# Sixteen MLP passes on one core: which second-layer products are cut in quarters, and the order of the sums around them

## The chip, the cores and the metric

The kernel runs on one core of a Trainium2 chip, as one launch. The metric is the device time in microseconds (us). A core has five engines that matter here, each with its own queue that is worked off in order: TensorE (PE, with its weight loads PEld), VectorE (DVE), ScalarE (ACT), GpSimd (POOL) and SyncE (SP, which issues most DMAs). They meet only through semaphores.

## The reference, cut to what matters

Eight samples of 512 tokens by 512 features go through four stages: a grid update, an attention block with its MLP, a mixture-of-experts MLP (one expert per sample) and a low-rank response. The change touches the two MLPs and what runs between them:

```python
h = _ln(x) * g2 + beta2
ff = _gelu2(h @ W1 + b1) @ W2 + b2          # x + ff, W1: 512 x 2048, W2: 2048 x 512
...
h = gelu(einsum('bsh,bhi->bsi', x, Wi[expert]) + bi[expert])
o = einsum('bsi,bih->bsh', h, Wo[expert]) + bo[expert]
y = layernorm(o + x) * gamma + beta
...
return hidden_states + strength * response  # strength: one number per sample; response: rank 32
```

All of it is in 32-bit floats.

## The kernel before, in words

The first half of the span is the grid and the attention. The second half is `mlp_stage` (L1198): 16 passes, `run(q, hooks)` for q = 0 to 15; 0 to 7 are the attention block's MLP for the eight samples, 8 to 15 the experts' MLP. Each pass multiplies with seven products in place of eight (Strassen's scheme in Winograd's form: sums of quadrants are formed first, then seven products of half size, then sums of the products).

**First layer**, steps 0 to 27: four groups g of 512 hidden features, seven products each (`L1`, L1592), every step one product. W's quadrant sums come from `w_quads` (L1570, POOL, four sums a group), the activations' from `b_staged` (L1510). The outcome lands in `acts`, and ACT applies the GELU in place.

**Second layer**, steps 28 to 55: seven products over all four groups, four steps each. Call the left quadrants of `acts` A and the right ones of `wo` B, with the sums S1 to S4 and T1 to T4. The order before is P1 = A00 B00 (28), P5 = S1 T1 (32), P2 = A01 B10 (36), P6 = S2 T2 (40), P7 = S3 T3 (44), P3 = S4 B11 (48), P4 = A11 T4 (52); in the last pass P3 and P7 change places, and P4 is done by rows for the kernel's end.

- `second` (L1784) does one product in halves: 16 matmuls that are 256 wide, into one PSUM bank. Before, P1, P5 and P6 go this way.
- `third` (L1802) does one product in quarters, with a second level of the same scheme: 28 matmuls that are 128 wide, into two banks (a and b), and an epilogue: ACT copies a piece of a to `yw`, DVE makes three sums in `yw`, ACT copies one piece to b, DVE adds `yw` to b. Before, P2, P7, P3 and P4 go this way. Each needs four sums on its left side (`l_sum`, L1665: DVE, with three copies by ACT into a staging bank, `stage`) and four on its right side (`r_sum`, L1654: POOL). `PLACES` (L1633) says in which quadrants of `acts` and `wo` its operands lie, `set_up` and `fresh` which buffers take the sums.
- `s13` and `t13` (L1614, L1888) form S1 and S3, T1 and T3. `t2s2` (L1698) forms T2 and S2 in place of T1 and S1, called behind each group of P5. `t4s4` (L1706) forms T4 in B00's place and S4 in A00's.

**The order of the work around the matmuls** is written out by hand: `hooks[s]` is a list of functions called when PE's program comes to step s. A hook fixes the place of its instructions in their own engine's queue; only data ties them to PE. Hooks registered earlier come first within a step. Those that `mlp_stage`'s loop registers (L2158 on) come before those of `run`.

**PSUM**: eight banks. Tag "u" has six (products of both layers and the small products `pf`, `pg`, `pz`, `po`), tag "tr" has two (all copies of `stage`).

**Side work in a pass.** Passes 0 to 7: four Gram-Schmidt steps, each `gs_norm` (DVE, a square root on POOL) and `gs_b` (DVE, then `gs_a`: POOL issues two DMAs that spread the next row, `qb`); the next sample's layer norm (`norm` at 21, `normed` at 31) and its transposes (`rows32` at 34 to 37), with `turn` at 38. Passes 9 to 15: the finishing of the pass before, `tail_norm` (5), `tail_normed` (9), transposes (14 to 20), `tail_spread` (28), `tail_scale` (34 to 37, ACT), `tail_gamma` (37, one DVE product over 2048 columns), `tail_feats` (38, `pf`), `gate` (39, `pg`), `strength` (41, `pz`, then ACT's sigmoid with a table load, then DVE), `add_beta` (42, DVE and four POOL sums), `tail_sum` (46, four `po` in four banks), `tail_add` (47 to 51, DVE).

**Loads**: `load_wo` (step 0, 4 MB), `load_wi` of groups 2 and 3 (step 0) and of the next pass's 0 and 1 (48 and 52), into the buffers x0 to x3, which between them hold the sums of the quartered products.

Of the kernel before, what the change touches and what calls it, by code (L numbers as in the profile page):

```python
# [11 lines left out]
F32 = mybir.dt.float32  # L12
# [8 lines left out]
NB = 8  # L21
# [1176 lines left out]
def mlp_stage(tc, a, small, xp, io, wo8, x1d, ident, eidx, sigs, layernorm, rstd_of, phalf, wl3, g2, b1, first):  # L1198
# [4 lines left out]
    with ExitStack() as ctx:  # L1203
# [211 lines left out]
        def norm(q):  # L1415
            st = small.tile([P, R, 6], F32, name=f"ln1_st_{q}", tag="ln1_st")
            mv = small.tile([P, R, 2], F32, name=f"ln1_mv_{q}", tag="ln1_mv")
            for r in range(R):
                pin(nc.vector.bn_stats(st[:, r, :], xs[q][:, r, :]))
                pin(nc.vector.bn_aggr(mv[:, r, :], st[:, r, :]))  # L1420
            norms[q] = mv, rstd_of(mv[:, :, 1], LN_EPS, R, "ln1", pin)

        def normed(q):
            mv, rs = norms.pop(q)
            h = [ap.tile([P, D], F32, name=f"h_{q}_{r}", tag="tmp", bufs=4) for r in range(R)]
            sh = small.tile([P, R], F32, name=f"ln1_s_{q}", tag="ln1_s")
            pin(
                nc.vector.scalar_tensor_tensor(sh, mv[:, :, 0], -1.0, rs, ALU.mult, ALU.mult)
            )
            for r in range(R):  # L1430
                pin(
                    nc.scalar.activation(
                        h[r], xs[q][:, r, :], AF.Identity, bias=sh[:, r : r + 1],
                        scale=rs[:, r : r + 1],
                    )
                )
            hs[q] = h

        blks = {}

# [154 lines left out]
        def run(q, hooks):  # L1595
# [26 lines left out]
            def fresh(*ks):  # L1622
# [8 lines left out]
                    hx[k] = v  # L1631

            PLACES = {  # L1633
                "p2": ((0, 1), (1, 0)), "p7": ((1, 0), (0, 1)), "p3": ((0, 0), (1, 1)),
                "p4": ((1, 1), (0, 0)),
            }

            def left(key, k, m):
# [26 lines left out]
            def l_sum(key, n):  # L1665
# [8 lines left out]
                else:  # L1674
                    add(s2, s1, st[key + "b"], sub)
                    add(s4, st[key + "c"], s2, sub)

            def set_up(part):
                if part == 0:
                    fresh(2)  # L1680
                    r_homes("p2", *hx[2])
                elif part == 1:
                    fresh(0, 1, 3)
                    l_homes("p2", *hx[3])
                    r_homes("p7", *hx[0][0:3])
                    r_homes("p3", *hx[1][0:3])
                elif part == 2:
                    fresh(2, 3)
                    l_homes("p7", hx[0][3], hx[1][3], hx[2][0])
                    r_homes("p4", *hx[2][1:4])  # L1690
                    l_homes("p3" if last else "p4", *hx[3][0:3])
                elif not last:
                    l_homes("p3", *(
                        io.tile([P, NG, P], F32, name=f"s4_{q}_{i}", tag=f"v{i}", bufs=2)
                        for i in range(3)
                    ))

            def t2s2(g):  # L1698
                if g < NG - 1:
                    stage(f"s2_{g + 1}", act_quad(g + 1, 0, 0))  # L1700
                else:
                    stage("s4_0", act_quad(0, 0, 1))
                gadd(ts[q, g], quad(wo[:, g], 1, 1), ts[q, g], ALU.subtract)
                add(ss[g], ss[g], st[f"s2_{g}"], ALU.subtract)

            def t4s4(g):  # L1706
                if g < NG - 1:
                    stage(f"s4_{g + 1}", act_quad(g + 1, 0, 1))
                gadd(quad(wo[:, g], 0, 0), quad(wo[:, g], 1, 0), ts[q, g], ALU.subtract)
                add(act_quad(g, 0, 0), st[f"s4_{g}"], ss[g], ALU.subtract)  # L1710

            tail, last = q > NB, q == NQ - 1
            four = (40, 41, 42), (44, 45, 46)
            for part, s in enumerate((25, 28, 40, 44)):
                at(hooks, s, set_up, part)
            for key, ss_, ts_ in (
                ("p2", (28, 29, 30), (25, 26, 27, 28)),
                ("p7", four[last], (29, 30, 31, 31)),
                ("p3", four[not last], (40, 40, 40, 40) if tail else (40, 41, 42, 43)),
                ("p4", (47, 48, 49), (44, 44, 44, 44) if tail else (43, 44, 45, 46)),  # L1720
            ):
                if key == "p4" and last:
                    continue
                for n_, s in enumerate(ss_):
                    at(hooks, s, l_sum, key, n_)
                for n_, s in enumerate(ts_):
                    at(hooks, s, r_sum, key, n_)
            for g in range(NG):
                at(hooks, 36 + g, t4s4, g)

            for g in range(NG):
                out = {
# [48 lines left out]
                        gelu(0)  # L1781


            def second(s, A, B, each=None):  # L1784
                y = ps.tile([P, 2, H], F32, name=f"y_{q}_{s}", tag="u", bufs=6)
                for g in range(NG):
                    go(s + g)
                    if s == 28 and g == 2:
                        stage(f"s13_{NG - 1}", act_quad(NG - 1, 1, 0))
                    if s == 28 and g == 3:  # L1790
                        s13(NG - 1)
                    for i in range(2):
                        for m in range(2):
                            mm(
                                y[:, m, :], A(g)[:, i, m * P : (m + 1) * P], B(g)[:, i, :],
                                g + i + m == 0, g + i + m == NG + 1,
                            )
                    if each:
                        each(g)
                return y  # L1800

            def third(s, key):  # L1802
# [14 lines left out]
                    a=((L(0, 0), M(0, 0)), (s2, t2), (s3, t3), (s1, t1)),  # L1817
                    b=((L(1, 0), M(1, 0)), (s4, M(1, 1)), (L(1, 1), t4)),
                )
                jobs = [(n, k, g, v) for n in "ab" for k, v in enumerate(four[n]) for g in range(NG)]  # L1820
                for i, (n, k, g, (A, B)) in enumerate(jobs):
                    if i % 7 == 0:
                        go(s + i // 7)
                    last = len(four[n]) - 1
                    mm(
                        ys[n][:, k, :], A[:, g, :], B[:, g, :], k + g == 0,
                        k == last and g == NG - 1,
                    )
                    if n == "a" and k == last and g == NG - 1:
                        pin(nc.scalar.copy(w[:, 0, :], y[:, 0, :]))  # L1830
                        add(w[:, 1, :], y[:, 1, :], w[:, 0, :])
                        add(w[:, 2, :], y[:, 2, :], w[:, 1, :])
                        add(w[:, 1:4:2, :], y[:, 3:4, :].to_broadcast([P, 2, P]), w[:, 1:3, :])
# [15 lines left out]
            p1 = second(28, lambda g: act_quad(g, 0, 0), b(0, 0))  # L1849
            pin(nc.scalar.copy(yu, p1))  # L1850
            x_add(0, 0, p1)
            stage("s2_0", act_quad(0, 0, 0))
            p5 = second(32, lambda g: ss[g], lambda g: ts[q, g], t2s2)
            x_add(1, 1, p5)
            x_add(0, 1, p5)
            p2 = third(36, "p2")
            x_add(0, 0, p2)
            p6 = second(40, lambda g: ss[g], lambda g: ts[q, g])
            add(p6, p6, yu)
            x_add(0, 1, p6)  # L1860
            pin(nc.scalar.copy(yu, p6))
# [8 lines left out]
            if q < NQ - 1:  # L1870
                p4 = third(52, "p4")
                x_add(1, 0, p4)
            else:
                for m in range(2):
                    y = ps.tile([P, H], F32, name=f"y_{q}_52_{m}", tag="u", bufs=6)
                    for g in range(NG):
                        if g % 2 == 0:
                            go(52 + 2 * m + g // 2)
                        for i in range(2):
                            mm(  # L1880
                                y, act_quad(g, 1, 1)[:, i, m * P : (m + 1) * P],
                                b(0, 0)(g)[:, i, :], g + i == 0, g + i == NG,
                            )
                    last_row(m, y)

# [272 lines left out]
        for q in range(NQ):  # L2158
# [18 lines left out]
            at(hooks, 7, w_quads, q, 2, gadd)  # L2177
            at(hooks, 14, w_quads, q, 3, gadd)
            for g in range(NG):
                at(hooks, 18 + 2 * g, t13, q, g)  # L2180
            if nx:
                if nx < NB:
                    at(hooks, 21, norm, nx)
                    at(hooks, 31, normed, nx)
                for r in range(R):
                    at(hooks, 34 + r, lambda r=r, n=nx: rows32(
                        n, r, hs[n][r] if n < NB else xs[n][:, r, :]
                    ))
                at(hooks, 38 if q <= NB else 40, turn, nx)
                if nx < NB:  # L2190
                    for c in range(KC):
                        at(hooks, 46 + c, scale, nx, c)
                at(hooks, 51, b_staged, nx)
                at(hooks, 51, w_quads, nx, 0, gadd)
# [13 lines left out]
            elif q > NB:  # L2208
# [6 lines left out]
                at(hooks, 28, tail_spread, o)  # L2215
                for c in range(KC):
                    at(hooks, 34 + c, tail_scale, o, c)
                at(hooks, 37, tail_gamma, o, every)
                at(hooks, 38, tail_feats, o, every)
                at(hooks, 39, gate, o)  # L2220
                at(hooks, 41, strength, o)
# [100 lines left out]
```

## Time and profile before

| | us |
|---|---|
| three runs | 2627.62, 2633.33, 2635.84 (median 2633.33) |
| the profiled execution | 2628.13 |
| its span, first to last instruction | 2626.3 |
| PE busy | 2586.3 (98%) |
| DVE busy | 2015.7 (77%) |
| POOL busy | 1753.4 (67%) |
| ACT busy | 1309.0 (50%) |

The granted TensorE clock is 0.996 of full speed. In a listing of groups a line gives the source line, the engine, the operation, the output and inputs by the program's names, the count and the busy time. In a timeline or a chain a line begins with the start in us and the duration; a bracket holds the idle time of the engine before it and what ended it. A 32-bit matmul shows as two records, so a product in halves is 32 records and one in quarters 56. `y` is a product in halves, `y_36a` and `y_36b` the banks of the quartered product that begins at step 36; `u` is the first layer; `q` and `s` among inputs are buffers of sums.

### The profile page before, as it was taken

What the parts mean: (1) busy time and instruction counts of PE and PEld (TensorE: products, weight loads), DVE (VectorE), ACT (ScalarE), POOL (GpSimd) and SP (SyncE); (2) the same over time, 40 slices, a digit from 0 to 9 for tenths busy, and PEclk for the clock granted to TensorE, in tenths of its full rate; (3) what the DMA queues carried; (4) which work ended last, traced back from release to release, by engine and by line L of the source; (5) the groups of instructions that cost most, each with busy time, mean ns of one, the idle gap of its engine ahead of it and who ended that gap; (6) DMA issues with size and microseconds to landing.
All of it is one profiled execution on the core that took longest, in us unless ns stands there. A gap on an engine that the chain in (4) does not pass through costs nothing.

```text
span 2626.3 us, 44146 instructions
## 1 busy us (share of the span) xinstructions
PE 2586.3 (98%) x15664; PEld 1962.4 (75%) x15664; DVE 2015.7 (77%) x3924; ACT 1309.0 (50%) x2743; POOL 1753.4 (67%) x1422
## 2 busy tenths in 40 slices
PE   6999999999999999999999999999999999999998
PEld 3455555555555555798999899899899899889897
DVE  7978798888888756588877778777567667667667
ACT  2676767676777766243344334333334434434433
POOL 4555565655555656488787887877676786776773
PEclk9999999999999999999999999999999999999999
DMA  9775766666767555544553563564345355256241
GB/s 330 255 235 182 262 200 236 217 230 217 250 222 241 171 165 197 145 135 101 167 181 71 153 197 78 128 191 141 112 155 189 101 185 199 91 185 208 83 169 44
DMA packets 242128, 460.60 MB, mean 175 GB/s; under 512 B 33936, under 2 KB 77528, under 8 KB 232822
## 3 DMA queue, kind: packets, MB, share of 16 engines
q1 hardware_dynamic: 238042, 447.04, 49.7%
q0 software_dynamic: 3552, 10.72, 4.2%
q8 instruction: 125, 2.05, 0.3%
q14 instruction: 93, 0.76, 0.1%
q10 hardware_dynamic: 316, 0.03, 0.0%
HBM read 398.43 MB, written 55.09 MB: 173 GB/s over the span
## 4 chain that ended last, share of the span: by engine, by line
PE 93%; DVE 2%; issue 2%; DMA 2%; ACT 1%; POOL 0%; SPq 0%; DVEq 0%; ACTq 0%; POOLq 0%
PE u L1211 29%; PE y L1211 13%; PE tr L564 8%; PE s L561 5%; PE pv L561 4%; PE ctx L561 4%; PE pk L561 4%; PE pq L561 4%; PE o L561 3%; PE y_44a L1211 2%; PE y_36a L1211 2%; PE y_48a L1211 2%; PE y_52a L1211 2%; PE y_36b L1211 2%; PE y_44b L1211 2%
## 5 line engine op out<-in xcount | busy, mean ns | idle before, releaser
L998 POOL TENSOR_TENSOR bt<-bt,mk 128x1024 f32<-128x1024 f32 x256 | 541.6, 2140 | 58.3 <-DMA bt<-in_bias 38.0
L1026 ACT ACTIVATE bt<-bt,mn 128x512 f32<-128x512 f32 x512 | 365.7, 718 | 78.7 <-DVE mn L1021 78.5
L564 PEld LDWEIGHTS tr<-ident,bt 128*128 128x128 f32 x2048 | 230.4, 141 | 148.8 <-issue 101.7
L1021 DVE CUSTOM_DVE_ANT_0 bt<-s,bt 128x512 f32<-128x512 f32 x512 | 329.7, 683 | 4.7 <-PE s L561 3.6
L1211 PE MATMUL u<-bt,wi 128*128 128x256 f32 x1440 | 330.5, 379 | 0.0
L1052 ACT COPY pt<-tr 128x512 f32<-128x512 f32 x376 | 207.6, 584 | 204.5 <-PE tr L564 196.6
L1211 PEld LDWEIGHTS u<-bt,wi 128*128 128x128 f32 x1440 | 272.4, 190 | 36.4
L1217 DVE TENSOR_TENSOR act<-u,u 128x512 f32<-128x512 f32 x256 | 174.7, 687 | 158.7 <-PE u L1211 121.1
L564 PE MATMUL tr<-ident,bt 128*128 128x128 f32 x2048 | 277.5, 278 | 7.7 <-ACT pt L1052 3.4
L1211 PE MATMUL u<-tb,ws 128*128 128x256 f32 x1024 | 242.3, 379 | 0.0
L1211 PE MATMUL y<-t,s 128*128 128x256 f32 x1024 | 228.1, 380 | 0.0
L1741 ACT ACTIVATE act<-act,b 128x512 f32<-128x512 f32 x128 | 84.1, 713 | 285.7 <-DVE act L1217 268.2
L1211 PEld LDWEIGHTS u<-tb,ws 128*128 128x128 f32 x1024 | 194.2, 190 | 26.8 <-issue 0.3
L1211 PEld LDWEIGHTS y<-t,s 128*128 128x128 f32 x1024 | 192.7, 190 | 25.6 <-issue 0.4
L1741 ACT ACTIVATE act<-act,bi 128x512 f32<-128x512 f32 x128 | 84.6, 713 | 244.1 <-DVE act L1217 244.1
L1050 DVE COPY pt<-tr 128x512 f32<-128x512 f32 x136 | 93.7, 689 | 133.6 <-PE tr L564 132.9
L561 PE MATMUL s<-kt,qt 32*128 32x512 f32 x1024 | 164.1, 640 | 1.0 <-ACT kt L651 0.8
L1217 DVE TENSOR_TENSOR u<-u,u 128x512 f32<-128x512 f32 x192 | 130.9, 682 | 43.7 <-PE u L1211 43.5
L1220 POOL TENSOR_TENSOR q<-wo,q 128x512 f32<-128x512 f32 x126 | 160.4, 1273 | 5.0
L1220 POOL TENSOR_TENSOR wo<-wo 128x512 f32<-128x512 f32 x111 | 143.3, 1291 | 8.7
L1220 POOL TENSOR_TENSOR t<-wo,t 128x512 f32<-128x512 f32 x64 | 80.9, 1279 | 101.0 <-PE y L1211 100.9
L1503 ACT COPY st_s<-act 128x512 f32<-128x512 f32 x192 | 111.9, 589 | 70.4 <-DVE s L1217 32.2
(443 smaller groups left out, 5604.9 us busy)
## 6 DMA issues: line engine op xcount, KB each, us to landing
bt<-in_bias SPq DMA_DIRECT2D x256, 512.0 KB
wo<-in_W SPq DMA_DIRECT2D x32, 1024.0 KB
wi<-in_Wi SPq DMA_DIRECT2D x32, 1024.0 KB
wo<-in_Wo_e SPq DMA_DIRECT2D x32, 1024.0 KB
wi<-in_W SPq DMA_DIRECT2D x28, 1024.0 KB
td<-tt SPq DMA_DIRECT2D x22, 1024.0 KB
bt<-td SPq DMA_DIRECT2D x176, 128.0 KB
gq<-coef_q SPq DMA_DIRECT2D x21, 512.0 KB
```

The costliest lines, as they stand in the source:

```text
L561: pin(nc.tensor.matmul(out, lhsT=lhsT, rhs=rhs, start=start, stop=stop))
L564: pin(nc.tensor.transpose(out, src, ident))
L998: nc.gpsimd.tensor_tensor(bt, bt, mask[b, r][:, None, :].to_broadcast([P, 2, S]), ALU.add)
L1021: nc.vector.tensor_tensor_reduce(bt[:, i, :], ss[h], bt[:, i, :], -1.0, 3.0e38, ALU.add, ALU.min, mn)
L1026: nc.scalar.activation(bt[:, i, :], bt[:, i, :], AF.Exp, bias=mn, scale=-1.0, accum_out=sums[b, c][:, h, r : r + 1],)
L1050: pin(nc.vector.tensor_copy(pt[:, :, r % 2, :], tr))
L1052: pin(nc.scalar.copy(pt[:, :, r % 2, :], tr))
L1211: pin(nc.tensor.matmul(out, lhsT=lhsT, rhs=rhs, start=start, stop=stop))
L1217: pin(nc.vector.tensor_tensor(out, x, y, op))
L1220: pin(nc.gpsimd.tensor_tensor(out, x, y, op))
L1503: pin(nc.scalar.copy(t, parts[0]))
L1741: nc.scalar.activation(acts[:, g, k, :], acts[:, g, k, :], func, bias=bi[:, j : j + 1])
```

## The change

- P6 is done in quarters by `third` (step 40); with P2, P7, P3 and P4 that makes five. P2 moves from 36 to 32, P5 from 32 to 36. The order is P1, P2, P5, P6, P7, P3, P4.
- S2 is written to A00's place and T2 to B00's (`s2` at 31 to 34, `t2` at 30 to 33); S4 to A01's and T4 to B10's (`s4` at 39 and 40, `t4` at 37 to 40). P6, P3 and P4 read them there.
- Buffers of the second-level sums are shared out anew (`set_up` in five parts, `free` for the buffers that S1 and T1 leave).
- In `third` the products of bank a come in the order 0, 2, 3, 1.
- POOL's list: `t13` at 10, 11, 16, 18 (before 18, 20, 22, 24); P2's right sums at 20 to 23 (before 25 to 28), P7's at 23 to 26 (before 29 to 31), P6's at 33 to 36, P3's at 40 to 43, P4's at 44 to 47; in passes 9 to 15 P3's at 40, 40, 41, 41 and P4's at 46, 46, 47, 48.
- `normed` is called by row at 33 to 36 (before all at 31); `tail_gamma` at 22 (before 37).

```diff
             PLACES = {
-                "p2": ((0, 1), (1, 0)), "p7": ((1, 0), (0, 1)), "p3": ((0, 0), (1, 1)),
-                "p4": ((1, 1), (0, 0)),
+                "p2": ((0, 1), (1, 0)), "p6": ((0, 0), (0, 0)), "p7": ((1, 0), (0, 1)),
+                "p3": ((0, 1), (1, 1)), "p4": ((1, 1), (1, 0)),
             }
...
-            def t2s2(g):
...
+            def t2(g):
+                o = quad(wo[:, g], 0, 0)
+                gadd(o, quad(wo[:, g], 1, 1), ts[q, g], sub)
+
+            def s2(g):
+                o = act_quad(g, 0, 0)
+                add(o, ss[g], st[f"s2_{g}"], sub)
                 if g < NG - 1:
                     stage(f"s2_{g + 1}", act_quad(g + 1, 0, 0))
...
+            def t4(g):
+                o = quad(wo[:, g], 1, 0)
+                gadd(o, o, quad(wo[:, g], 0, 0), sub)
+
+            def s4(*gs_):
+                for g in gs_:
+                    o = act_quad(g, 0, 1)
+                    add(o, st[f"s4_{g}"], act_quad(g, 0, 0), sub)
...
-            for part, s in enumerate((25, 28, 40, 44)):
+            for part, s in enumerate((20, 28, 36, 40, 44)):
                 at(hooks, s, set_up, part)
+            for g in range(NG):
+                at(hooks, 30 + g, t2, g)
+                at(hooks, (37, 37, 38, 39)[g] if tail else 37 + g, t4, g)
             for key, ss_, ts_ in (
-                ("p2", (28, 29, 30), (25, 26, 27, 28)),
-                ("p7", four[last], (29, 30, 31, 31)),
-                ("p3", four[not last], (40, 40, 40, 40) if tail else (40, 41, 42, 43)),
-                ("p4", (47, 48, 49), (44, 44, 44, 44) if tail else (43, 44, 45, 46)),
+                ("p2", (28, 29, 30), (20, 21, 22, 23)),
+                ("p6", (36, 37, 38), (33, 34, 35, 36)),
+                ("s4", (), ()),
+                ("p7", four[last], (23, 24, 25, 26)),
+                ("p3", four[not last], (40, 40, 41, 41) if tail else (40, 41, 42, 43)),
+                ("p4", (47, 48, 49), (46, 46, 47, 48) if tail else (44, 45, 46, 47)),
             ):
+                if key == "s4":
+                    at(hooks, 30, stage, "s2_0", act_quad(0, 0, 0))
+                    for g in range(NG):
+                        at(hooks, 31 + g, s2, g)
+                    at(hooks, 38, s4_stage, 0, 1)
+                    at(hooks, 39, s4, 0, 1)
+                    at(hooks, 39, s4_stage, 2, 3)
+                    at(hooks, 40, s4, 2, 3)
+                    continue
...
-            for g in range(NG):
-                at(hooks, 36 + g, t4s4, g)
...
+                turns = dict(a=(0, 2, 3, 1), b=(0, 1, 2))
...
-            stage("s2_0", act_quad(0, 0, 0))
-            p5 = second(32, lambda g: ss[g], lambda g: ts[q, g], t2s2)
+            p2 = third(32, "p2")
+            x_add(0, 0, p2)
+            p5 = second(36, lambda g: ss[g], lambda g: ts[q, g])
             x_add(1, 1, p5)
             x_add(0, 1, p5)
-            p2 = third(36, "p2")
-            x_add(0, 0, p2)
-            p6 = second(40, lambda g: ss[g], lambda g: ts[q, g])
+            p6 = third(40, "p6")
             add(p6, p6, yu)
...
-                at(hooks, 18 + 2 * g, t13, q, g)
+                at(hooks, (10, 11, 16, 18)[g], t13, q, g)
             if nx:
                 if nx < NB:
                     at(hooks, 21, norm, nx)
-                    at(hooks, 31, normed, nx)
+                    for r in range(R):
+                        at(hooks, 33 + r, normed, nx, r)
...
-                at(hooks, 37, tail_gamma, o, every)
+                at(hooks, 22, tail_gamma, o, every)
```

## The prediction

> **What bounds the kernel now.** I read the page's shares and chain first, then the chain in order of time, then the timelines of the engines in one middle pass (1356 to 1455 us) and one late pass (2021 to 2122 us).
>
> ```profile
> PE 93%; DVE 2%; issue 2%; DMA 2%; ACT 1%; POOL 0%; SPq 0%; DVEq 0%; ACTq 0%; POOLq 0%
> ...
> 1356.86 48.35 PE u L1211 x224
> 1405.21 13.81 PE y L1211 x64
> 1419.02 3.57 PE y_36a L1211 x32
> 1422.59 2.68 PE y_36b L1211 x24
> 1425.27 6.91 PE y L1211 x32
> ```
>
> PE sets the end: 93% of the chain. A pass is 48.35 us of first layer and seven second-layer products one behind the other, with no gap. A product in halves (y) is 32 matmul records in 6.91 us, 216 ns each; one in quarters (y_36a with y_36b) is 56 in 6.25 us, 111.6 ns each. Passes 1 to 7 take 94.08 us (1356.86 to 1450.94), passes 9 to 14 take 97.67 (2021.73 to 2119.39): there pf, pg, pz and po of the pass before are let in, and again PE has no gap. So nothing is to be won but matmul time; anything late on DVE, ACT or POOL can only add.
>
> **The gain.** P6 goes from halves to quarters: 6.91 - 6.25 = 0.66 us, in all 16 passes 10.6 us. The four other quartered products, P1 and P5 keep their records; only their order changes. The sums for S2, T2, S4 and T4 keep their number too (four of each a pass, DVE and POOL): they go to other places at other steps, and the last pass's last product reads T4 from its new place.
>
> The Trainium skill, "TensorE: Matmul & The Clock Gate", Back-to-back issue gap, speaks against quarters: the spacing of matmuls with weight loads falls only from 131 ns at width 512 to 81 at 128. Read linearly (an estimate from that page) 128 would cost 0.83 of 256, so 56 records 10.0 us, and the change would lose 3.1 us a pass, 50 us in all. The rows above have 0.517 and decide.
>
> **What the extra quarters cost elsewhere.** Per pass four POOL sums (1.28 us each), four DVE sums on the left (0.60 apart), three ACT copies, and the epilogue: an ACT copy, three DVE sums (1.07), an ACT copy, a DVE sum (0.56). DVE gets 4.0 us more behind the first layer. Between its first p2 sum and its last x sum the middle pass has 44 us with about 6.4 idle, the late pass 49 with about 7. That fits on paper; whether it stalls is a matter of order, so I laid the queues out by hand, in program order, with the rows' durations. Zero is 48.35 us before a pass's first second-layer matmul (1356.69 and 2021.56).
>
> **Late passes.** PSUM has six "u" banks. At step 46 four po tiles are taken while P7 holds two, so every bank of P6 must be free by then. P6 had one bank; now its second bank is held until yu is copied out of it.
>
> ```profile
> 2094.10 1.28 ACT L2020 ACT_TABLE_LOAD   x1
> 2095.39 0.26 ACT L2020 ACTIVATE st<-pz,gb 128x1 f32<-128x1 f32 x1
> 2095.69 0.16 DVE L1217 TENSOR_TENSOR st<-st,sigs 128x1 f32<-128x1 f32 x1 [1.03 <-ACT st L2020]
> ...
> 2099.41 0.70 DVE L1217 TENSOR_TENSOR y<-y,yu 128x512 f32<-128x512 f32 x1 [0.28 <-PE y L1211]
> 2100.14 0.69 DVE L1217 TENSOR_TENSOR x<-y,x 128x512 f32<-128x512 f32 x1
> 2100.92 0.59 ACT L1861 COPY yu<-y 128x512 f32<-128x512 f32 x1 [3.26 <-DVE x L1217]
> ...
> 2102.43 1.14 PE L1211 MATMUL po<-rw,ft 32*128 32x512 f32 x8
> ```
>
> Before, P6's bank is free at 2101.51 and po starts at 2102.43: 0.9 us to spare. After: P5 ends at 68.43 plus pf 1.1 and pg 0.81, so 70.34; P6 takes 6.25 and pz 0.14, to 76.73; step 46 is half of P7 later, 79.85, and its third po at 80.4. DVE: two x sums from 70.5, then s4 of groups 2 and 3, to 73.03. Only then does ACT get the staging bank for p7b (0.6), then the table load (1.28) and the sigmoid: 75.25. DVE waits for it in order at st, and behind it stand s1, s3, beta, s2, s4 (3.2 us, to 78.5), P6's three sums (79.5), an ACT copy (0.3), the sum to y (0.6), with yu (0.74), x (0.7), and ACT's yu copy: 82.5. PE waits 2.1 us. P3's first bank needs P7's three sums, which end at 86.75 with P7's matmuls over at 86.3: 0.45 more. I take 2.5 us a pass, in seven passes 17.6; bounds 0.8 (DVE a microsecond and a half earlier) and 3.5. The gamma product (2.29 us of DVE, 0.59 of ACT), moved from 37 to 22, is already out of this count: in the first layer of a late pass DVE waits on PE again and again (0.97 and 1.03 us at the end of it), so it costs nothing there; without that cover it would sit in front of p2's sums.
>
> The Trainium skill, "ScalarE: Activation LUTs", What ACT_TABLE_LOAD costs, adds a drain of 1.38 us to 1.28 of load. The trace has the load 0.02 us behind the copy before it and the sigmoid 1.29 later, so no drain; by the page the stall would be 3.9 us and the seven passes 9.7 us dearer.
>
> **Middle passes.** P2 now runs straight behind P1, at 55.27 and not 62.18; its second quarter needs s3 at 56.16.
>
> ```profile
> 1390.54 1.04 POOL L1259 DMA_DIRECT2D qb<-qm  x2 [1.93 <-DVE qm L1277]
> ...
> 1397.33 1.04 POOL L70 TENSOR_TENSOR ln_r<-ln_v,mhalf 128x4 f32<-128x4 f32 x1 [3.10 <-DVE ln_v L68]
> ...
> 1404.28 0.53 POOL L1243 TENSOR_TENSOR gs_d<-gn_s,phalf 64x1 f32<-64x1 f32 x1
> ...
> 1400.14 1.37 DVE L1236 CUSTOM_DVE_ANT_0 junk_gn<-qb 64x512 f32<-64x512 f32 x1
> ...
> 1411.16 0.68 DVE L1217 TENSOR_TENSOR q<-act,st_p2a 128x512 f32<-128x512 f32 x1
> ...
> 1452.96 0.74 DVE L1277 SCALAR_TENSOR_TENSOR qm<-qb,al,qm 64x512 f32<-64x512 f32 x1
> ```
>
> The row of 1411.16 is s3; it ends 55.15 after the pass's zero: 1.0 us to spare if DVE keeps its time. It stands behind the Gram-Schmidt steps (gs), whose roots and qb broadcasts are on POOL's list. That list had gaps (1.93, 3.10); the new one has none: t13 of groups 0 and 1 (5.1 us) stands before w_quads 3, t13 of 3 before gs_a of step 18, p2's four and p7's first sum before the root of step 24. From gs_a of step 55 at 3.1 the sums run 4.2, 9.2, 15.0, 21.0, 22.1, 27.1, 32.2, 37.9, and qb of step 18 is issued at 37.9 instead of 33.9 and lands some 5.7 us behind its first issue, near 44.4 (second issue); DVE wanted it at 43.45. That is 1.0 late, all the margin. And DVE, with 4.0 us more to do, ends the pass later: by my list the qm of step 55, 2.9 us into the next pass before, ends at 4.7; POOL's list starts with the gs_a that waits for it, has no gap, and hands these 1.8 us to the qb of step 18 and so to s3. P2 waits 0 to 2.5 us; P4, whose s3 came 2.0 us early (DVE done at 86.7, wanted at 88.7), waits 0 to 0.8. I take 1.2 + 0.4, the value between, as part of the lag may be taken up where DVE idles on PE (1.04 and 0.49 us in that half). Passes 1 to 7: 11.2 us; bounds 0 and 23. Passes 0 and 8 have no such lag; they keep 0.66.
>
> P6's left sums (done near 67.4 for 69.3), p7's and p3's (2 us early), all right sums on POOL (p6's second near 61 for 69.3) hide. The wo transfer (4 MB, DMA idle again some 20 us into a pass) is just there for t13 at 22; if it isn't, w_quads 3, done at 32.2 for 39.7, has 7 us. Moving norm's scaling to 33 to 36 puts one ACT operation between copies and is in the list.
>
> **Sum.** -10.6 + 17.6 + 11.2 = +18.2 us on the profiled execution's 2628.1: 2646. That execution is 5.2 us below the median of the three times, 2633.3; for the median I add it: 2651.
>
> **Rivals.** (1) Only the late passes stall: -10.6 + 17.6 = +7.0, 2640. For it: p2's sums have a microsecond now, and a lag on DVE may dissolve in the first layer. Against: POOL's list without gaps. (2) Nothing stalls, and all of the matmul time is won: 2633.3 - 10.6 = 2623. For it: by the idle time above DVE keeps 2 to 3 us free behind the first layer. Against: six banks, and nothing takes the sigmoid off DVE's way. It decides if DVE reaches P6's last sum 2 us sooner than I count. (3) The lag of the middle passes isn't taken up at all: 2.5 + 0.8 us in seven of them, 23 us, and 3.5 in late ones: -10.6 + 23 + 24.5, 2670. (4) The change doesn't do what it says: t13 waits for wo, w_quads 3 comes late for step 23, and PE stalls in the first layer. It needs 7.5 us of delay; near 2665 with 3 us in eight passes. Little speaks for it.
>
> **Chances.** My forecast 0.42, (1) 0.25, (2) 0.20, (3) 0.09, (4) 0.04. About 0.3%, 7.9 us, can be told from no change. (2) is just past that bound on the faster side; (1) is within it for the most part. So faster 0.22, same 0.19, slower 0.59. The likeliest case's own range is 2640 to 2664; the range from (2)'s side to (3)'s, 2621 to 2671.
>
> **What would show it.** y_40a and y_40b in place of y: 6.25 us. A gap of PE inside po of the late passes, released by ACT's yu copy or DVE's x sum; y_48a waiting for DVE. In middle passes a gap in y_32a released by DVE's q or act of p2, and junk_gn waiting for qb. No gap in either: rival 2. The prediction fails if late passes come in under 97.7 us.

## The result: 2.2% slower, and the profile after

| | before | after |
|---|---|---|
| median of six runs each, us | 2631.99 (2627.62 to 2635.84) | 2690.34 (2686.40 to 2693.53) |
| the profiled execution, us | 2628.13 | 2691.52 |
| its span, us | 2626.3 | 2688.8 |
| PE busy, us | 2586.3 | 2597.8 |

The ratio is 1.022, with an interval of 1.0206 to 1.0235. The forecast had the side right and the size wrong: 2651 us with a range to 2671, so the change cost 58 us where I had 18.

Cut at the start of each pass's first second-layer product (P1 to P1), the spans differ by 62.5 us (the profiled executions lie 3.9 us below and 1.2 us above their medians, so it is a little more than between these):

| stretch | before | after | difference | forecast |
|---|---|---|---|---|
| up to the first P1 | 1122.56 | 1129.75 | +7.19 | 0 |
| passes 0 to 7 | 755.61 | 795.59 | +39.98 | +5.9 |
| pass 8 | 94.08 | 93.43 | -0.65 | -0.66 |
| passes 9 to 14 | 586.01 | 599.43 | +13.42 | +11.1 |
| last P1 to the end | 68.08 | 70.62 | +2.54 | +1.8 |

Pass 8, which has neither Gram-Schmidt steps nor a tail, shows the change as it would be without stalls: 0.65 us won. The difference is 44 us more than the forecast's 18; 34 of them lie in passes 0 to 7, and 7 ahead of them.

The chain of waits, by engine, of the changed kernel:

```profile
PE 66%; DVE 14%; POOL 7%; ACT 4%; DMA 4%; issue 3%; SPq 1%; DVEq 0%; ACTq 0%; POOLq 0%
```

PE had 93% before. The chain now leaves PE for DVE, for POOL and for the qb transfers. The list of waits on PE (who waited for whom: us in total, times, the longest) names the places; the four largest that belong to the MLP are

```profile
PE y L1211 <- ACT act L1777: 26.1, 7, 5.3
...
PE y_48a L1211 <- DVE yw L1217: 9.7, 7, 1.4
PE y_44b L1211 <- ACT yu L1892: 7.3, 7, 1.3
...
PE y_40a L1211 <- DVE q L1217: 2.7, 1, 2.7
```

The second and third line are the two waits in late passes that the prediction named, by what ends them; but the one for `yu` stands at P7's second bank, behind po, and not inside po. The first is one that I didn't foresee: `y` waiting for the GELU is P1, not P2. The fourth is in pass 0, where P6 waits for its left sums.

**A middle pass.** P1's fourth group needs the last two GELUs of the first layer, its first four records only the first of them. In the trace before, DVE, ACT and PE in the pass whose zero is 1356.69:

```profile
1407.33 0.74 DVE L1277 SCALAR_TENSOR_TENSOR qm<-qb,al,qm 64x512 f32<-64x512 f32 x1
1408.00 0.68 DVE L1217 TENSOR_TENSOR act<-u,u 128x512 f32<-128x512 f32 x1
...
1408.71 1.33 ACT L1741 ACTIVATE act<-act,b 128x512 f32<-128x512 f32 x2 [1.56 <-DVE act L1217]
...
1405.04 7.07 PE L1211 MATMUL y<-wo,act 128*128 128x256 f32 x32
```

One GELU takes 0.72 us, so the first ends at 1409.43 and the second at 1410.04. P1 begins at 1405.04 and reaches its fourth group after three quarters of 6.91 us, at 1410.22. The margin was 0.8 us, with no gap to show it. After, with the pass's zero at 1480.29, the rows of POOL, DVE, ACT and PE:

```profile
1521.26 1.04 POOL L1259 DMA_DIRECT2D qb<-qm  x2
...
1527.69 1.08 DVE L1236 CUSTOM_DVE_ANT_0 junk_gn<-qb 64x512 f32<-64x512 f32 x1 [0.67 <-DMA qb<-qm]
...
1531.55 0.53 POOL L1243 TENSOR_TENSOR gs_d<-gn_s,phalf 64x1 f32<-64x1 f32 x1
...
1533.63 0.93 DVE L1276 TENSOR_TENSOR al<-al,below 64x1 f32<-64x1 f32 x1
1534.60 1.84 DVE L1277 SCALAR_TENSOR_TENSOR qm<-qb,al,qm 64x512 f32<-64x512 f32 x1
1536.37 0.67 DVE L1217 TENSOR_TENSOR act<-u,u 128x512 f32<-128x512 f32 x1
...
1537.07 1.33 ACT L1777 ACTIVATE act<-act,b 128x512 f32<-128x512 f32 x2 [2.65 <-DVE act L1217]
...
1528.63 5.34 PE L1211 MATMUL y<-wo,act 128*128 128x256 f32 x24
1537.85 2.46 PE L1211 MATMUL y<-wo,act 128*128 128x256 f32 x8 [3.88 <-ACT act L1777]
1540.10 1.92 PE L1211 MATMUL y_32a<-wo,act 128*128 128x128 f32 x8
1541.81 3.25 PE L1211 MATMUL y_32a<-q,q 128*128 128x128 f32 x24
```

Read from the top: qb is issued 41.0 us into the pass (33.9 before), DVE starts the third Gram-Schmidt step 47.4 in (43.45 before), the step's last operation takes 1.84 us (0.74 before), and the last sum ahead of the GELU begins 56.1 in (51.3 before), 4.8 us late. PE goes on at 1537.85, when the first of the two GELUs is done and the second is not; it has stood 3.88 us, about the 4.8 less the margin. The windows of that stretch (the first number is the length, then each engine's busy time; the column behind POOL is the granted clock) show a second cost:

```profile
1534.00:1538.00 4.00, 0.15 (x1) 0.15 (x2) 3.00 (x3) 1.35 (x3) 3.07 (x5) 1.00 0.13 5
1538.00:1542.00 4.00, 4.00 (x17) 3.66 (x18) 2.96 (x5) 2.89 (x6) 4.00 (x4) 0.65 0.81 28
1542.00:1546.00 4.00, 4.00 (x35) 4.00 (x34) 3.93 (x7) 2.44 (x5) 3.92 (x4) 0.92 0.02 4
```

Behind the wait the granted clock is 0.65 and then 0.92. The eight records of P1's last group take 2.25 us in place of 1.73, the first bank of P2 4.79 in place of 3.57: 1.74 us more. So a pass loses 3.88 + 1.74, and wins 0.65; this one came out 5.3 us longer than before.

**A late pass**, PE:

```profile
2050.63 1.14 PE L1211 MATMUL po<-rw,ft 32*128 32x512 f32 x8
2051.70 0.71 PE L1211 MATMUL y_44a<-q,q 128*128 128x128 f32 x4
2053.40 1.16 PE L1211 MATMUL y_44b<-wo,act 128*128 128x128 f32 x8 [0.99 <-ACT yu L1892]
...
2057.74 2.02 PE L1211 MATMUL y_48a<-wo,act 128*128 128x128 f32 x16 [1.39 <-DVE yw L1217]
```

P6's second bank and P7's sums are both late. 2.38 us of waits; the pass takes 99.90 us where it took 97.67.

### The profile page after: what moved, and what is told of

Its sections match the earlier page's. It is cut to its first block, busy times and chain, and to the rows that moved or that the text cites. A ratio compares the mean times of both kernels' runs of the same rounds, so it can differ in the third digit from the quotient of the medians.

```text
span 2688.8 us, 45287 instructions
## 1 busy us (share of the span) xinstructions
PE 2597.8 (97%) x16048; PEld 1974.6 (73%) x16048; DVE 2120.0 (79%) x4052; ACT 1343.9 (50%) x2823; POOL 1840.4 (68%) x1486
## 4 chain that ended last, share of the span: by engine, by line
PE 66%; DVE 14%; POOL 7%; ACT 4%; DMA 4%; issue 3%; SPq 1%; DVEq 0%; ACTq 0%; POOLq 0%
PE u L1211 17%; PE tr L564 8%; PE s L561 5%; PE y L1211 5%; PE ctx L561 4%; PE pv L561 4%; PE o L561 4%; PE pk L561 4%; PE pq L561 4%; POOL ws L1220 2%; DVE q L1217 2%; DVE act L1217 2%; DMA qb<-qm 2%; DVE x L1217 1%; PE y_32a L1211 1%
## 5 line engine op out<-in xcount | busy, mean ns | idle before, releaser
L1220 POOL TENSOR_TENSOR wo<-wo 128x512 f32<-128x512 f32 x175 | 222.0, 1280 | 8.2
L1220 POOL TENSOR_TENSOR ws<-wi 128x512 f32<-128x512 f32 x60 | 76.7, 1278 | 120.5 <-DMA wi<-in_W 60.7
L1211 PE MATMUL y<-wo,act 128*128 128x256 f32 x544 | 128.3, 393 | 26.1 <-ACT act L1777 26.1
L1211 PEld LDWEIGHTS y<-wo,act 128*128 128x128 f32 x544 | 105.8, 196 | 43.6 <-ACT act L1777 29.0
L1220 POOL TENSOR_TENSOR q<-wo,q 128x512 f32<-128x512 f32 x96 | 124.6, 1298 | 3.8
```

Source lines behind the costliest of these rows:

```text
L1211: pin(nc.tensor.matmul(out, lhsT=lhsT, rhs=rhs, start=start, stop=stop))
L1220: pin(nc.gpsimd.tensor_tensor(out, x, y, op))
```

## The experiments

Every ratio below is to the kernel before, run beside it on the same chip (its medians there were 2631.6 to 2632.7).

**e1: POOL's list as before.** Only three lines of places go back.

```diff
-            at(hooks, (10, 11, 16, 18)[g], t13, q, g)
+            at(hooks, 18 + 2 * g, t13, q, g)
-                ("p2", (28, 29, 30), (20, 21, 22, 23)),
+                ("p2", (28, 29, 30), (25, 26, 27, 28)),
-                ("p7", four[last], (23, 24, 25, 26)),
+                ("p7", four[last], (29, 30, 31, 31)),
```

> The changed kernel with POOL's first-layer list as before: t13 at 18, 20, 22, 24, P2's right sums at 25 to 28, P7's at 29 to 31. Nothing is left out. Theory A (the list without gaps hands every delay to the qb broadcast of step 18, and so to the last GELU): passes 1 to 7 go from 98.6 to 101.1 us back under 95, PE's wait in P1 for the GELU goes, and the time falls by 32 to 42 us, to 2648 to 2658. Rival B (DVE's 4 us of added sums behind the first layer make the lag, whatever POOL's order): passes 1 to 7 stay above 97.5, the time falls by less than 15 us. Passes 9 to 15 stay at 99.9 either way.

2659.42 us, 1.0099 (1.0081 to 1.0118): 31 us come back, just short of theory A's 32, with the products, their order and the number of sums unchanged. Passes 1 to 6 take 94.84 to 95.42 us, late ones 99.9 as after. Waits on PE, in the same view:

```profile
PE y_48a L1211 <- DVE yw L1217: 9.7, 7, 1.4
PE y_44b L1211 <- ACT yu L1892: 7.3, 7, 1.3
PE y_52a L1211 <- DVE act L1217: 4.7, 6, 0.8
...
PE y_40a L1211 <- POOL q L1220: 3.4, 1, 3.4
```

P1's wait is gone, the late ones are as they were. New in sight: 0.8 us in P4 of a middle pass, and 3.4 in pass 0, which grew from 98.9 to 100.6 us. In one pass the last sum ahead of the GELU begins 0.8 us later than before (52.12 us in), and P1 still shows no wait: the margin again.

**e2: no Gram-Schmidt steps** in the changed kernel (the hooks of `gs_norm`, `gs_b` and the first `gs_a` left out; so the low-rank part starts from rows that aren't made orthogonal).

> The changed kernel without the 32 Gram-Schmidt steps (gs_norm, gs_b and the first gs_a are left out, so the low-rank basis isn't orthonormal). Theory A: with no qb to wait for, DVE keeps its time, passes 1 to 7 come to 93.4 us and pass 0 near 94, the time falls by 40 to 50 us, to about 2645. Rival B: DVE also loses some 12 us of work a pass, so it can't be told from A here; a third theory C (the wait for the GELU comes from the sums themselves, not from the Gram-Schmidt steps) would leave the 3.9 us wait in P1. Passes 9 to 15 stay at 99.9.

2640.02 us, 1.0035 (1.0024 to 1.0047). Passes 0 to 6 take 93.43 us each, with no wait on PE; late passes stay at 99.9. Without the Gram-Schmidt steps the new order, POOL's new list and the quarters of P6 cost nothing in passes 0 to 8. Whether it is the steps' chain that does, or only their work on DVE and POOL, this run can't tell; e1 and e6, which keep all of that work, speak for the chain.

**e3 and e4: `po` split** over steps 46, 46, 49 and 50, in the changed kernel (e3) and in e1 (e4), so that po doesn't ask for four banks at once.

```diff
-                    at(hooks, 46, tail_sum, o, r)
+                    at(hooks, (46, 46, 49, 50)[r], tail_sum, o, r)
```

> The changed kernel with the four po products of passes 9 to 15 at steps 46, 46, 49, 50 and not all at 46, so that two banks are enough at 46. Theory A (P6's second bank, held until yu is copied, makes PE wait inside po, and P7's bank at the start of P3): passes 9 to 14 go from 99.9 to 97.0 to 97.8, the time falls by 14 to 20 us. Rival (the wait is DVE's backlog, and only moves to P3 or P4): passes 9 to 14 stay above 99. Passes 1 to 7 as in the changed kernel.

> Both edits, POOL's old first-layer list and the split po. If both theories hold they add up: 2690 - 37 - 16 is about 2637, and if nothing at all is late the 10.6 us of matmul time are left as a gain against the kernel before: 2622. If the DVE lag stays at the end of the passes: 2640 to 2650.

2689.95 us, 1.0214 (1.0197 to 1.0231), and 2654.70, 1.0088 (1.0071 to 1.0104). Both waits left the list, and yet a late pass still took 99.5 us: the split gained 0.4 where 2.4 of waits had gone. That was a miss, and it looked like a wrong theory. The rows of e4, PE and its weight loads, show where it went:

```profile
2114.68 1.13 PE L1211 MATMUL po<-rw,ft 32*128 32x512 f32 x4
2115.73 0.71 PE L1211 MATMUL y_44a<-q,q 128*128 128x128 f32 x4
...
2120.62 1.12 PE L1211 MATMUL po<-rw,ft 32*128 32x512 f32 x2
2121.67 0.49 PE L1211 MATMUL y_48a<-wo,act 128*128 128x128 f32 x2
...
2115.73 0.52 PEld L1211 LDWEIGHTS y_44a<-q,q 128*128 128x128 f32 x4 [0.76 <-issue]
```

A product of po is two records. A group of one product takes 1.05 us of PE's time from start to start, one of two products the same, and one of four 1.07 in the rows of after above. The products of a group run side by side: of after's eight records four start at 2050.63 to 2050.65 and four at 2051.16 to 2051.18. So a group costs about as much as one product alone, and a split pays that again: three groups in place of one are 2.1 us more. How much of the 1.05 is the change from one kind of product to the other isn't shown.

**e5: the cause of the late waits taken away, po left whole.** In e1's late passes DVE stands for the sigmoid in the middle of P6's work:

```profile
2015.98 0.16 DVE L1217 TENSOR_TENSOR st<-st,sigs 128x1 f32<-128x1 f32 x1 [2.23 <-ACT st L2051]
```

```diff
             pin(nc.scalar.activation(st, pz, AF.Sigmoid, bias=gb2))
-            add(st, st, sigs[:, q - NB : q - NB + 1], ALU.mult)
+            if also:
+                add(st, st, sigs[:, q - NB : q - NB + 1], ALU.mult)
...
             x, st, beta = xs[q], outs[q]["st"], extra[q][1][2]
+            add(st, st, sigs[:, q - NB : q - NB + 1], ALU.mult)
...
-                at(hooks, 42, add_beta, o)
+                at(hooks, 44, add_beta, o)
```

> The old list of e1_pool_old, and in the late passes DVE's multiplication by sigs and the sum to beta moved from steps 41 and 42 to 44, behind P6's epilogue. Theory A (the two waits of a late pass, 1.0 us for yu and 1.4 us for yw, come from DVE standing 2.2 us for the sigmoid; splitting po took them away too but paid about 1.05 us for each extra group of po): both waits go, po stays one group, late passes 97.4 to 97.7 us instead of 99.9, in all 2641 to 2647 us. Rival B (the time is in TensorE's own stream, since splitting po took the waits away and gained 0.4): late passes stay at 99.4 to 99.9, 2656 to 2660 us. Middle passes as in e1_pool_old, 94.8 to 95.4.

2645.70 us, 1.0045 (1.0031 to 1.0059); late passes 97.67 to 97.95. The wait of `y_44b` is gone, that of `y_48a` is 3.4 us in seven passes where it was 9.7. Theory A holds in the main; it had both waits gone.

**e6: the same kind of cure for the middle passes.** DVE stood 1.25 us in every pass (0.4 in e5's late ones) for P3's staging copies, which ACT makes behind the copy to `yu`; they go ahead of it. In pass 0, P7's right sums and T4 go behind P6's right sums.

```diff
-                ("p3", four[not last], ...
+                ("p3", four[0] if last else (43, 45, 46), ...
-                ("p7", four[last], (29, 30, 31, 31)),
+                ("p7", four[last], (29, 30, 31, 31) if q else (36, 37, 38, 39)),
-                at(hooks, (37, 37, 38, 39)[g] if tail else 37 + g, t4, g)
+                at(hooks, (37, 37, 38, 39)[g] if tail else 37 + g if q else 40, t4, g)
```

> As e5_st_late, with P3's staging copies at step 43 ahead of the yu copy (DVE stood 1.25 us for them in every pass), and in pass 0 P7's right sums and T4 behind P6's right sums on POOL. Theory A (what is left of passes 1 to 7 is two waits of 0.55 and 0.79 us for left sums that are late by DVE's idle time before them; pass 0's wait of 3.4 us is POOL's order): middle passes 93.4 to 93.7, pass 0 94 to 96, in all 2625 to 2634 us, so no slower than before. Rival B (DVE has too much work in a middle pass, whatever its order): middle passes stay at 94.8, 2637 to 2642 us.

2630.81 us, 1.000 (0.999 to 1.0009). Passes 1 to 6 take 93.42 to 93.51 us: every one of them has 0.57 to 0.66 of the gain, with all of DVE's work in it. Pass 0 missed its figure, 97.26. In two late passes a load is 0.4 us late instead, in the rows of POOL, SP and PE:

```profile
2006.46 4.97 POOL L1220 TENSOR_TENSOR x<-x,beta 128x512 f32<-128x512 f32 x4 [6.62 <-DVE beta L2059]
...
2011.46 0.36 SPq L1395 DMA_DIRECT2D beta<-in_beta  x1
...
2023.18 3.69 PE L1211 MATMUL u<-bt,wi 128*128 128x256 f32 x16 [0.41 <-DMA wi<-in_Wi]
```

SP issues the next pass's beta only when POOL is through with the old one, 0.03 us after its last sum, and the next wi stands behind it on SP's list.

**e7 and e8: which part of POOL's list.** The changed kernel, with either only the sums of P2 and P7 back (e7: the second and third pair of e1's diff) or only t13 back (e8: the first pair). In e8 part of P7's right sums are formed before t13 has put T3 into the quadrant that they read; their number is the same.

> The changed kernel with only P2's and P7's right sums back at 25 to 28 and 29 to 31; t13 stays early. Theory A (what counts is how many of POOL's sums stand before the root of step 24): the root comes 3 to 4 us sooner, P1's fourth group waits 0 to 1 us, middle passes 94.8 to 96.5, in all 2655 to 2669 us. Rival B (the early t13 makes the qb of step 18 late, and that alone decides): middle passes 98 to 99.5, 2682 to 2692 us.

> The changed kernel with only t13 back at 18, 20, 22 and 24; P2's and P7's right sums stay early. Theory A (the sums before the root of step 24 count, and t13 now joins them there): no better, middle passes 98 to 101, in all 2682 to 2698 us. Rival B (the early t13 makes the qb of step 18 late): qb is issued some 5 us sooner, P1's fourth group doesn't wait, middle passes 94.8 to 96.5, 2655 to 2669 us.

e7 2665.01 us, 1.0121 (1.0102 to 1.0141), middle passes 96.0 (the first 97.7); e8 2706.19, 1.0280 (1.0259 to 1.0301), middle passes 100.7 to 101.8, worse still than theory A had it. The two rows that tell most are when DVE has `gn_s` ready and when POOL takes the root. First e7, then e8:

```profile
1515.52 0.07 DVE L1236 DVE_READ_ACCUMULATOR2_ANT gn_s<- 64x1 f32 x1
...
1515.68 0.93 POOL L1243 TENSOR_TENSOR gs_d<-gn_s,phalf 64x1 f32<-64x1 f32 x1 [2.71 <-DVE gn_s L1236]
```

```profile
1533.75 0.07 DVE L1236 DVE_READ_ACCUMULATOR2_ANT gn_s<- 64x1 f32 x1
...
1541.75 0.54 POOL L1243 TENSOR_TENSOR gs_d<-gn_s,phalf 64x1 f32<-64x1 f32 x1
```

In e7 POOL is waiting when DVE is ready; in e8 POOL comes 7.9 us late, six sums of 1.3. In e8 the qb of step 18 is issued some 34 us into the pass, about as before, and PE waits 5.2 us in P1 all the same; in e7 it is as late as after (about 41), and P1 waits 1.9 us in the first middle pass and 0.5 in the others. So a late qb costs little where POOL is free for the root, and sums ahead of the root cost much with qb in time. The changed kernel has the late qb, and POOL comes to the root 2.8 us behind `gn_s` (1528.71 to 1531.55), just as it does in the kernel before (1401.44 to 1404.28). So its lag of 4.8 us is 4.0 from qb, and the rest is `qm`, 1.1 us longer, less 0.3 elsewhere. In e7 POOL takes the root 0.2 us behind `gn_s` and `qm` takes 0.74 us, which wins back some 3.4 us.

**e9: what e6 still lost.** `load_extra` behind the next wi, and pass 0's third `gs_b` behind P6's left sums.

```diff
-                    at(hooks, 45, load_extra, nx)
+                    at(hooks, 49, load_extra, nx)
-                third = (24, 27) if q else (28, 31)
+                third = (24, 27) if q else (28, 39)
```

> As e6_best, with the late passes' load_extra at step 49 instead of 45 (SP's list stood there for POOL's last sum with beta, and the load of wi behind it came 0.4 us late for the next first layer), and in pass 0 the third gs_b at step 39 instead of 31, behind P6's left sums. Theory A (these two waits are what e6_best has lost): late passes 97.0 to 97.4 us instead of 97.2 to 97.8, pass 0 93.8 to 95.5 instead of 97.3, since the wait of 2.0 us also costs the granted clock behind it; in all 2622 to 2629 us, faster than before by 0.1 to 0.35%. Rival B (in pass 0 DVE is simply full): the wait goes to P7 or P3, pass 0 stays at 96 to 97.3, 2628 to 2631 us.

2627.21 us (2624.42 to 2633.52, eleven runs), 0.9979 (0.9970 to 0.9988). It beats both kernels, the one before by 0.2%. Late passes take 97.17 us, six times alike. Pass 0 takes 96.41: the wait in P6 fell from 2.0 to 0.4 us and one of 1.3 came up in P7, both for DVE's sums, so there DVE seems to be full, and rival B is nearer.

**e10: the price of a second group of po**, in e9 (46, 46, 49, 49).

> As e9_extra_gs, but the four po in two groups, at 46, 46, 49 and 49. Theory A (each further group of 32-row products costs TensorE about 1.05 us, which is why splitting po gained so little): late passes 1.0 to 1.1 us longer than e9_extra_gs's, in all 6 to 7 us more. Rival B (splitting po moved a wait that the records don't show, and costs nothing by itself): late passes within 0.3 us of e9_extra_gs's.

2633.64 us, 1.0007 (0.9998 to 1.0016); late passes 98.26, 1.08 us above e9's. In this kernel PE waits for nothing in them, so the 1.08 is the group's own price.

## Why the prediction was wrong, by its own steps

- **Gain, 0.66 us a pass: right.** 0.65 in pass 8 and in e2's middle passes, 0.57 to 0.66 in e6's. In e9's late passes 0.50 is left; the other 0.15 wasn't traced.
- **Late passes, 17.6 us in seven: right in mechanism, a little small.** Net of the gain I had +13.0, measured +16.0. I put 2.1 us on po and 0.45 on P3's bank; the waits are 1.0, behind po, and 1.4. e5 shows that DVE's stand for the sigmoid, which I had named, is the cause.
- **POOL's list without gaps makes qb late: right, and too small.** I had the issue at 37.9 us, or 39.7 with the 1.8 handed on from the pass before (measured: 1.8); it came at 41.0. (The 5.7 us that I gave to its landing are those of the second issue, 5.71 before and 5.75 after; from the first issue it is 6.3, which gives about the 44.4 that I used.)
- **Middle passes, 11.2 us: the step that failed.** I had qb late by 1.0 + 1.8 = 2.8 us, took P2's s3 as the one that waits, with a margin of 1.0 us, let part of the lag be taken up, and reckoned 1.2 + 0.4 us a pass. Nothing was taken up: in the pass shown DVE starts the step 4.0 us late and ends it 4.8 late. The first consumer of the late DVE is P1's fourth group, through the last two GELUs, with a margin of 0.8; it waits 3.9. Gross of the gain, passes 1 to 7 cost 39.9 us in place of 11.2. I had looked for margins only where the order changed; P1 stayed in its place, and so I never asked what it needs. That moved the wait, but hardly its size, since the two margins differ by 0.2; the size came from the lag. P4's 0.4 to 0.8 came in two passes only.
- **Two prices that were missing in that step.** The first is DVE and POOL holding each other up. `qm` has a median of 744 ns before, 1731 after and 744 in e1, in 32 rows each; single sums of POOL take 1.6 to 1.73 us in place of 1.27, six of them ahead of the late qb in the pass shown where three do before. That is 1.2 us, about what its issue comes later than I had it. I had used the durations of a POOL with gaps for one without. The second is the clock behind a long wait, 1.74 us in the pass shown; behind the shorter waits of passes 3 and 7 (3.07 and 2.23 us) it stayed at 1.00.
- **Pass 0 "keeps 0.66": wrong.** It lost 4.6 us, 2.7 of them in the wait for P6's left sums, and about 2.4 more in its first layer, where `u` waited for DVE. The other 4.8 us ahead of the first P1 lie in front of the MLP, in code that is the same in both. There the same code moves by several us from run to run: the first P1 stood at 1132.39 in e9's profile and at 1123.46 in e10's.
- **P6's sums, P3's, wo and the gamma product hide: so in passes 1 to 15, but for 0.5 us once in P3; not in pass 0,** where P6's left sums came 2.7 us late. No wait on wo or gamma is in the list. The gamma move was not undone by itself.
- **Rivals.** (1) fell, since middle passes did stall. (2), nothing stalls, became true only with the places moved: e9 is at 2627 with pass 0 still held back. (3) had the right place to look, a lag that isn't taken up, but with 0.8 and 2.5 us for the waits. (4) didn't occur.

The Trainium skill, "SBUF — State Buffer", SBUF: two separate sides, states a rule that speaks against this change and that I had left out: a DVE instruction with two inputs from SBUF and a GpSimd instruction that reads SBUF exclude each other for their whole length. The rows agree: `qm` has both inputs there, and in pass 0 of e1 the 64x1 product `al`, 151 ns at its shortest, takes 4.22 us while POOL runs one sum behind the other. What the lock adds to a stretch hangs on how full POOL is there, so it is a function of the order and not of the instruction alone.

## What to carry to other kernels

When an engine's list is laid out anew, look for every consumer of what comes late on it, the ones that aren't moved included, and write down each margin; the smallest decides, and a zero gap in the trace doesn't say whether the margin is 0.8 us or 5. Then follow the lag to the end of its chain: here the margins were 0.8 and 1.0 us, and the lag, 4.8 us where I had 2.8, set the size. Put a short instruction on which a chain hangs (a root, a DMA's issue) ahead of bulk work in its queue, not behind it: in e8 six sums in front of one root left PE waiting 5.2 to 5.5 us in P1 in six passes. And price a stretch with durations from a stretch that is as full: the same instruction took 0.74 and 1.84 us.

## What was not expected of the hardware

- **The clock behind a wait.** After 3.88 us of waiting the granted clock was 0.65 over the next 4 us. A wait of 2.0 us was enough in e6's pass 0, in windows as above:

```profile
1146.00:1150.00 4.00, 2.03 (x16) 1.82 (x15) 3.86 (x8) 1.87 (x5) 3.92 (x4) 0.97 0.31 131
1150.00:1154.00 4.00, 4.00 (x24) 4.00 (x24) 3.94 (x7) 2.42 (x5) 3.92 (x4) 0.61 0.49 176
```

  The clock is 0.61 behind the wait, and 24 records took 4.54 us in place of 2.84. Behind waits of 1.0 and 1.4 us in the late passes it stayed at 1.00. The Trainium skill, "TensorE: Matmul & The Clock Gate", Part 1: The HAM clock gate, has a halved clock after an idle window of some 3.4 us; by the row of e6 a shorter wait can do it too. But waits of 2.23 and 3.07 us in passes 7 and 3 of the changed kernel left it at 1.00 over the next 4 us, so the length alone doesn't decide; what does isn't shown.
- **A group of 32-row products between 128-row ones** costs PE 1.05 to 1.08 us, with one, two or four products in it: they run side by side, and splitting the group pays the price again.
